# Conv stage of a two-layer network: four images side by side, tap tiles written back over three batches, logits in four column groups, last batch scaled by two engines

## The chip, the cores and the metric

The kernel runs on one core of one Trainium2 chip. The time is device microseconds from start to end of one execution. PE is the matrix engine (PEld its weight loads), DVE the vector engine, ACT the scalar engine, POOL the general one, SP the engine that issues most DMA transfers. A core has 16 DMA engines that carry the transfers of all queues.

## The reference

Two layers run after each other on x of 32 images, 128 channels, 56x56 pixels, all float32. The change lies in the first part of layer 0, up to the logits.

```python
x = jax.lax.conv_general_dilated(input, dw_kernel, (1, 1), ((3, 3), (3, 3)), feature_group_count=C, ...) + dw_bias
x = jnp.transpose(x, (0, 2, 3, 1))
mu = x.mean(-1, keepdims=True)
var = x.var(-1, keepdims=True)
x = (x - mu) / jnp.sqrt(var + 1e-06) * ln_gamma + ln_beta
xf = x.reshape(T, C)
logits = xf @ Wg + bg                 # 8 experts
topv, topi = jax.lax.top_k(logits, K) # K = 2
...
```

The tokens are then sorted by their weight, sent to experts of limited capacity (two matrix products with a gelu between), and added back. Layer 1 (a 3x3 depthwise convolution beside a scan over the pixels of each image, and two 1x1 convolutions) takes most of the time and is not changed.

## The kernel before, in words

The kernel is written for a framework that traces the program, orders each engine's instructions by a simulated greedy schedule, and places the semaphores itself. So the text of the program gives priorities, and the order on an engine can differ from it; once placed, each engine and each queue works strictly in that order. A pool with `bufs=n` gives each tile name n buffers; the (n+1)th use waits until the first is free. The conv stage has a pool `wp` (one buffer) and a pool `cp` (two, unless a tile says otherwise); in PSUM there are three buffers for `pc`, two for `p_in`, two for `p_xa`, one for `p_lg`.

The stage works on batches of four images (NB0 = 4, eight batches). A depthwise 7x7 convolution is turned into matrix products: two image rows (112 pixels, TT) of one channel lie along the partitions, 28 such row pairs (NP) and one of padding lie in the free dimension, and for each channel four 112x112 Toeplitz matrices made from the 49 taps are the weights.

- The taps are laid into `xt` among zeros and written to `taps_d` in DRAM (L337, L338). Only then is `xt` free for the first image.
- `fill(b, i)` (L341) loads one image into `xt` (L344, one buffer), turns it on PE, two rows at a time (L349), and copies four turned pairs at once on ACT into `slots2[b % 2]` (L351). All four images of batch 0 are filled ahead of the first convolution; those of batch b+1 are filled in the midst of batch b.
- `conv(b, c0)` (L353) does four channels: 16 matrix products (L379), each of them two passes in float32, and one addition of the bias on DVE (L383). The Toeplitz tiles `toep` hold two channels each and have five buffers. In batch 0 each is made from `raw`, which two transfers read from `taps_d` with overlapping rows (L361), by a copy on ACT (L368), and is written to `toep_d` in DRAM from POOL's queue (L369). `raw` shares the tag and the three buffers of `xa`. In batches 1 to 7 it is read from `toep_d` in one transfer (L371).
- `norm(b, i, q)` (L388) does seven of the 28 row pairs of one image, 16 times a batch, on the batch before the one being convolved: statistics over the channels on DVE (L396, L398), the root on ACT (L400), reciprocal and shift on DVE (L401, L403), seven scalings on ACT into `xa` (L406), gamma and beta on POOL (L409, L410), the store (L412), the turning of seven pieces on PE (L420), two copies on ACT into `xc_lg` (L422), then seven products with `xc_lg` as weights and the eight columns of `wg` streamed (L424), two passes each, and one addition of `bg` on DVE into the logits `lg` (L428).
- `top2(b)` (L430) finds the two best experts of a batch on DVE.

The last loop, at the end of the stage, mixes these: `conv` for all 32 groups of four channels, and between them the work list of norms, fills and one top2, spread evenly. The batch loop has one round more than there are batches: in it the last batch is normalized with no convolution beside it.

After the stage come the routing (to about 1.9 ms), the experts, and layer 1, which is bound by POOL's multiplications (L1330). Two lines of layer 1 serve only as prices: L1256 and L1284 are matrix products on four 64x64 quarters of the array.

## Time and profile before

Ten runs lie between 15733.27 and 15753.77 us.

| | us |
|---|---|
| median of ten runs | 15742.19 |
| profiled execution, its own time | 15740.14 |
| its span | 15738.4 |
| of it, conv stage up to the last logits | 1531 |
| ACT scalings L406 in the conv stage, 896 | 500.9 busy, 643 ns each |
| products of the logits L424, 1792 passes | 233.6 busy |
| Toeplitz copies L368, 64 | 60.0 busy, 943 ns each |

The profile gives for each engine its instructions with start and duration, and for idle time what ended it. In the rows "x" is a count, "<-" names what was waited for, and in the table of windows each engine has its busy time in a window followed by its number of instructions, then the TensorE clock granted (1 is full speed), the mean busy share of the 16 DMA engines, and what they moved. A matrix instruction's duration overlaps those of its neighbours, so a rate is read from the distance between starts. "q" after an engine's name is its sequencer, which issues transfers.

### The profile page before, as it was taken

To read this page: it belongs to the slowest core of one execution; us is meant where nothing else is said; L and a number is where in the kernel's file an instruction comes from. 1 tells how busy PE (TensorE), PEld (TensorE's weight loads), DVE (VectorE), ACT (ScalarE), POOL (GpSimd) and SP (SyncE) were. 2 spreads that over 40 slices of the span, in tenths; PEclk is the share of its full clock that TensorE was granted. 3 is DMA by queue.
4 is the path that set the end of the run, shared out by engine and by line. 5 is a ranking of instruction groups with operands and counts; after the bars stand their busy time and mean duration, and the time that the engine had idled before them with its cause. 6 is when DMAs were issued, how large, how long until landed. Compare 5 with 4: busy or idle time off the path is not lost. (4 is left out here: it accounts for less than half of the span.)

```text
span 15738.4 us, 249145 instructions
## 1 busy us (share of the span) xinstructions
PE 12846.1 (82%) x92981; PEld 7181.9 (46%) x92981; DVE 11109.1 (71%) x11254; ACT 10410.5 (66%) x20982; POOL 13461.5 (86%) x8122
## 2 busy tenths in 40 slices
PE   7996200003999989999999999999999999999998
PEld 7996100002777754444444444444444444444444
DVE  2655400000111149999999999999999999999999
ACT  4564200001444458888888888888888888888887
POOL 2443377777888879999999999999999999999999
PEclk9997555556999999999999999999999999999999
DMA  8785533333555545555555555555555555555555
GB/s 265 231 236 171 204 104 104 104 104 71 72 70 72 70 105 183 185 183 182 182 182 182 184 183 181 183 183 182 185 184 181 181 183 182 185 183 183 182 182 169
DMA packets 1239277, 2572.34 MB, mean 163 GB/s; under 512 B 139352, under 2 KB 676784, under 8 KB 1230384
## 3 DMA queue, kind: packets, MB, share of 16 engines
q1 hardware_dynamic: 1041584, 2361.95, 47.9%
q0 software_dynamic: 196480, 194.45, 7.3%
q8 instruction: 732, 11.99, 0.3%
q14 instruction: 481, 3.94, 0.1%
HBM read 2180.44 MB, written 375.43 MB: 162 GB/s over the span
## 5 line engine op out<-in xcount | busy, mean ns | idle before, releaser
L1330 POOL TENSOR_TENSOR db<-du,bb 128x896 f32<-128x896 f32 x3584 | 6843.6, 1940 | 0.1
L1343 ACT ACTIVATE da<-dt,aneg 128x449 f32<-128x449 f32 x7168 | 4540.2, 637 | 387.8 <-DVE r L1093 112.9
L1361 DVE TENSOR_TENSOR_SCAN da<-da,db 128x898 f32<-128x898 f32 x2240 | 4523.3, 2019 | 1.8 <-ACT da L1343 1.1
L1284 PE MATMUL py<-prod,ident 64*64 64x448 f32 x28672 | 3240.2, 548 | 178.7 <-DVE prod L1381 133.9
L1381 POOL TENSOR_TENSOR prod<-hs,cb 128x896 f32<-128x896 f32 x1344 | 2605.7, 1939 | 184.5 <-DVE r L1093 78.2
L1381 DVE TENSOR_TENSOR prod<-da,cb 128x896 f32<-128x896 f32 x2240 | 2440.2, 1089 | 202.7 <-DMA cb<-bc_d 88.3
L952 ACT COPY xc<-ept 128x512 f32<-128x512 f32 (+1 forms) x248 | 144.1, 581 | 2743.0 <-PE ept L950 2743.0
L858 POOL DMA_INDIRECT buf_d<-xg,slot x1568 | 1521.3, 970 | 484.9 <-issue 476.4
L910 POOL DMA_INDIRECT res_d<-ys,xb x984 | 1591.9, 1618 | 332.3 <-issue 287.1
L1361 DVE TENSOR_TENSOR_SCAN hs<-da,db 128x898 f32<-128x898 f32 x896 | 1785.7, 2014 | 0.1
L1284 PEld LDWEIGHTS py<-prod,ident 64*64 64x64 f32 x28672 | 1018.1, 132 | 1633.6 <-issue 883.1
L950 PE MATMUL ept<-ident,xb 128*128 128x128 f32 (+1 forms) x984 | 188.7, 274 | 1853.5 <-DMA xb<-buf_d 1853.5
L1124 PE MATMUL p_xm<-te,wk 128*128 128x448 f32 x3584 | 1395.4, 540 | 0.0
L902 DVE TENSOR_TENSOR ys<-py,b2t 128x512 f32<-128x512 f32 (+2 forms) x256 | 170.9, 670 | 1680.3 <-PE py L896 1663.3
L855 DVE COPY xg<-gate 128x28 f32<-128x28 f32 x56 | 11.5, 210 | 1749.1 <-DMA buf_d<-xg,slot 1749.1
L896 PEld LDWEIGHTS py<-w2t,hh 128*128 128x128 f32 x7872 | 936.2, 191 | 175.6 <-issue 113.4
L896 PE MATMUL py<-w2t,hh 128*128 128x128 f32 x7872 | 985.0, 278 | 0.3
L1124 PEld LDWEIGHTS p_xm<-te,wk 128*128 128x128 f32 x3584 | 671.7, 189 | 665.6 <-issue 567.7
L950 PEld LDWEIGHTS ept<-ident,xb 128*128 128x128 f32 (+1 forms) x984 | 124.6, 143 | 1857.0 <-issue 1856.6
L379 PE MATMUL pc<-xc,toep 112*112 112x112 f32 (+1 forms) x8192 | 940.2, 271 | 35.8 <-ACT toep L368 31.1
L1365 DVE TENSOR_TENSOR_SCAN hs<-da,db 128x449 f32<-128x449 f32 x896 | 927.3, 1077 | 0.8 <-POOL prod L1381 0.6
L1256 PE MATMUL p_l<-xh,dwd 64*64 64x224 f32 x16128 | 907.3, 352 | 22.1 <-ACT dt L1238 3.6
(240 smaller groups left out, 20138.2 us busy)
## 6 DMA issues: line engine op xcount, KB each, us to landing
bb<-bc_d SPq DMA_DIRECT2D x1792, 448.0 KB
cb<-bc_d SPq DMA_DIRECT2D x1792, 448.0 KB
toep<-toep_d SPq DMA_DIRECT2D x448, 392.0 KB
xg<-res_d SPq DMA_DIRECT2D x56, 1792.0 KB
buf_d<-zero SPq DMA_DIRECT2D x28, 2275.0 KB
xb<-buf_d SPq DMA_DIRECT2D x240, 260.0 KB
xt<-in_x SPq DMA_DIRECT2D x32, 1568.0 KB
res_d<-xa SPq DMA_DIRECT2D x128, 392.0 KB
```

What stands on the lines that cost most here:

```text
L379: nc.tensor.matmul(pc[:, c, :, lo:hi], lhsT=tp[c // 2][:, c % 2, 6 - 2 * o : 8 - 2 * o, :], rhs=s4[:, c, :, lo + o - 1 : hi + o - 1], star ...
L858: apart(nc.gpsimd.indirect_dma_start(out=buf_d[:, :], out_offset=bass.IndirectOffsetOnAxis(ap=slots[k][:, o + j : o + j + 1], axis=0), in_ ...
L896: nc.tensor.matmul(py[:n, j, :], lhsT=hh[:, k, j * 128 : j * 128 + n], rhs=w2t[:, k, :], start=k == 0, stop=k == KF - 1,)
L910: apart(nc.gpsimd.indirect_dma_start(out=res_d[:, :], out_offset=bass.IndirectOffsetOnAxis(ap=xb[:n, j, C + 1 : C + 2].bitcast(I32), axis= ...
L1124: nc.tensor.matmul(p[:, :CH1], lhsT=s["wk"][:, k, hs], rhs=d["te"][:, k : k + CH1], start=k == 0, stop=k == DC - 1 and not first,)
L1256: nc.tensor.matmul(d["p_l"][r][k * HD : (k + 1) * HD, : CH1 // 2], lhsT=s["dwd"][rs, t, rs], rhs=d["xh"][rs, dy + k * R : dy + (k + 1) * R ...
L1284: nc.tensor.matmul(ps[r][h * HD : (h + 1) * HD, :CH1], lhsT=lhsT(rs, h), rhs=rhs[rs, h, :], start=start, stop=stop,)
L1330: nc.gpsimd.tensor_tensor(dbv[i][:, :, 1:], st[g]["du"], units[u].pop("bb"), ALU.mult)
L1343: e = nc.scalar.activation(da[:, h * W1 : (h + 1) * W1], st[g]["dt"][:, h, :], AF.Exp, scale=s["aneg"][:, h, i : i + 1])
L1361: nc.vector.tensor_tensor_scan(hs, da, dbs[i], 0.0, ALU.mult, ALU.add)
L1365: half(u, h, nc.vector.tensor_tensor_scan(hs2[h][:, hh], da[:, hh], dbs[i][:, hh], 0.0, ALU.mult, ALU.add))
L1381: eng.tensor_tensor(w["prod"], w["hs"][0][:, :, 1:], w["cb"], ALU.mult)
```

## The change

Four things change in the conv stage.

- The two slot tiles become full 128-partition tiles `whole`. The second is not needed until batch 1 is filled, so it first holds the four images of batch 0 side by side (`begin`) and, behind them, the taps (`tapf`). `xt` serves batches 1 to 7. The zeros are set by DVE, not by POOL. The four image loads no longer wait for each other, and the first stands ahead of the write of `taps_d`. The loads of `wg` and of the rows follow behind them.
- `PACKED = (0, 44, 88, C)`: batch 0 builds all 64 tiles from `raw` but writes back only the first 22 (channels 0 to 43); batch 1 reads these 22 and builds 42 from `raw`, of which it writes back 22; batch 2 reads 44 and builds 20, writing all of them back. From batch 3 all are read. `raw` has its own name in the pool, with the pool's two buffers; `xa` keeps three.
- The logits: `wg` is padded with zeros to 32 columns and becomes the weights. The turned pieces lie in one tile `turns` (one buffer, an eighth piece of zeros). Four products, each of two pieces (224 columns), go to partitions 0, 32, 64 and 96 of one PSUM tile. ACT copies them to `lt`, PE turns them back in two transposes, and DVE adds `bg` with a rearranged view. `lg` has one column more and one buffer.
- In the last batch, three of the seven scalings of a norm (odd j) are done by DVE as one two-operation instruction.

```diff
@@ -309,8 +309,33 @@
             tc.tile_pool(name="po1", bufs=2, space=PSUM) as pot,
             tc.tile_pool(name="pl1", bufs=1, space=PSUM) as plg,
         ):
-            wg = wp.tile([C, E], F32, name="wg")
-            nc.sync.dma_start(out=wg, in_=a["L0_conv_Wg"])
+            SH = NP + 1
+            PAD = (HW + 2) * HW
+            whole = [wp.tile([128, C * NB0 * SH], F32, name=f"xc{i}") for i in range(2)]
+            slots2 = [t[:TT].rearrange("p (c j) -> p c j", c=C) for t in whole]
+            taps_d = dram.tile([C, TR * TS], F32, name="taps_d")
+            toep_d = dram.tile([TT, C, 8, HW], F32, name="toep_d")
+            tapf = whole[1][:, NB0 * PAD : NB0 * PAD + TR * TS]
+            nc.vector.memset(tapf, 0.0)
+            taps = tapf.rearrange("c (y x) -> c y x", x=TS)
+            dwk = a["L0_conv_dw_kernel"].rearrange("c o h w -> (c o) h w")
+            for y in range(7):
+                nc.sync.dma_start(out=taps[:, 7 - y, 52:59], in_=dwk[:, y, :])
+            begin = whole[1][:, : NB0 * PAD].rearrange("c (i n) -> c i n", i=NB0)
+            xt = wp.tile([C, PAD], F32, name="xt")
+            for v in (begin, xt.unsqueeze(1)):
+                nc.vector.memset(v[:, :, :HW], 0.0)
+                nc.vector.memset(v[:, :, HW + L :], 0.0)
+            nc.sync.dma_start(out=begin[:, 0, HW : HW + L], in_=x_d[0])
+            nc.sync.dma_start(out=taps_d, in_=tapf)
+            for i in range(1, NB0):
+                nc.sync.dma_start(out=begin[:, i, HW : HW + L], in_=x_d[i])
+            wg = wp.tile([C, 32], F32, name="wg")
+            nc.vector.memset(wg, 0.0)
+            nc.sync.dma_start(out=wg[:, :E], in_=a["L0_conv_Wg"])
+            turns = wp.tile([C, 8, TT], F32, name="xc_lg")
+            nc.vector.memset(turns[:, 7, :], 0.0)
 
             def rows(v, n, name):
                 t = wp.tile([TT, n], F32, name=name)
@@ -322,41 +347,31 @@
             lng = rows(a["L0_conv_ln_gamma"], C, "lng0")
             lnb = rows(a["L0_conv_ln_beta"], C, "lnb0")
 
-            taps_d = dram.tile([C, TR * TS], F32, name="taps_d")
-            toep_d = dram.tile([TT, C, 8, HW], F32, name="toep_d")
-            slots2 = [wp.tile([TT, C, NB0 * (NP + 1)], F32, name=f"xc{i}") for i in range(2)]
-            xt = wp.tile([C, (HW + 2) * HW], F32, name="xt")
-            nc.gpsimd.memset(xt, 0.0)
-            taps = xt[:, : TR * TS].rearrange("c (y x) -> c y x", x=TS)
-            dwk = a["L0_conv_dw_kernel"].rearrange("c o h w -> (c o) h w")
-            for y in range(7):
-                nc.sync.dma_start(out=taps[:, 7 - y, 52:59], in_=dwk[:, y, :])
-            nc.sync.dma_start(out=taps_d, in_=xt[:, : TR * TS])
-            nc.gpsimd.memset(xt[:, :HW], 0.0)
             def fill(b, i):
 
                 n = b * NB0 + i
-                nc.sync.dma_start(out=xt[:, HW : HW + L], in_=x_d[n])
+                if b > 0:
+                    img = xt
+                    nc.sync.dma_start(out=xt[:, HW : HW + L], in_=x_d[n])
+                else:
+                    img = begin[:, i, :]
                 for j0 in range(0, NP + 1, 4):
                     w = min(4, NP + 1 - j0)
                     p = pin.tile([TT, 4, C], F32, name="p_in")
                     for j in range(w):
-                        nc.tensor.transpose(p[:, j, :], xt[:, (j0 + j) * TT : (j0 + j + 1) * TT], ident)
+                        nc.tensor.transpose(p[:, j, :], img[:, (j0 + j) * TT : (j0 + j + 1) * TT], ident)
                     o = i * (NP + 1) + j0
                     nc.scalar.copy(slots2[b % 2][:, :, o : o + w], p[:, :w, :].rearrange("p j c -> p c j"))
+            PACKED = (0, 44, 88, C)
 
             def conv(b, c0):
 
                 tp = []
                 for c in range(c0, c0 + 4, 2):
                     t = cp.tile([TT, 2, 8, HW], F32, name="toep", bufs=5)
-                    if b == 0:
-                        raw = cp.tile([TT, 2, 8, TS], F32, name="raw", tag="xa", bufs=3)
+                    if b < len(PACKED) - 1 and c >= PACKED[b]:
+                        raw = cp.tile([TT, 2, 8, TS], F32, name="raw")
                         for r in range(2):
                             nc.sync.dma_start(
                                 out=raw[r * HW : (r + 1) * HW].rearrange("k c y x -> k c (y x)"),
@@ -366,7 +381,8 @@
                                 ),
                             )
                         nc.scalar.copy(t, raw[:, :, :, :HW])
-                        nc.gpsimd.dma_start(out=toep_d[:, c : c + 2], in_=t)
+                        if c < PACKED[b + 1]:
+                            nc.gpsimd.dma_start(out=toep_d[:, c : c + 2], in_=t)
                     else:
                         nc.sync.dma_start(out=t, in_=toep_d[:, c : c + 2])
                     tp.append(t)
@@ -401,38 +417,55 @@
                 nc.vector.reciprocal(rs, rs)
                 nm = cp.tile([TT, w], F32, name="nm")
                 nc.vector.scalar_tensor_tensor(nm, mv[:, :, 0], -1.0, rs, ALU.mult, ALU.mult)
-                xa = cp.tile([TT, 2 * 8 * TS], F32, name="xa", bufs=3)[:, : w * C].rearrange("p (j c) -> p j c", c=C)
+                xa = cp.tile([TT, w, C], F32, name="xa", bufs=3)
                 for j in range(w):
-                    nc.scalar.activation(
-                        xa[:, j, :], xv[:, :, j], AF.Identity, bias=nm[:, j : j + 1], scale=rs[:, j : j + 1]
-                    )
+                    if b == NB - 1 and j % 2:
+                        nc.vector.tensor_scalar(
+                            xa[:, j, :], xv[:, :, j], rs[:, j : j + 1], nm[:, j : j + 1], ALU.mult, ALU.add
+                        )
+                    else:
+                        nc.scalar.activation(
+                            xa[:, j, :], xv[:, :, j], AF.Identity, bias=nm[:, j : j + 1], scale=rs[:, j : j + 1]
+                        )
                 nc.gpsimd.tensor_tensor(xa, xa, lng.unsqueeze(1).to_broadcast([TT, w, C]), ALU.mult)
                 nc.gpsimd.tensor_tensor(xa, xa, lnb.unsqueeze(1).to_broadcast([TT, w, C]), ALU.add)
                 col = (b * NB0 + i) * TPI + q * w
                 nc.sync.dma_start(
                     out=res_d[col * TT : (col + w) * TT, :].rearrange("(k p) c -> p k c", p=TT), in_=xa
                 )
-                pl = plg.tile([TT, w, E], F32, name="p_lg")
                 for j0 in range(0, w, 4):
                     g = min(4, w - j0)
                     p = pot.tile([C, 4, TT], F32, name="p_xa")
                     for j in range(g):
                         nc.tensor.transpose(p[:, j, :], xa[:, j0 + j, :], ident[:TT, :TT])
-                    xc = cp.tile([C, 4, TT], F32, name="xc_lg")
-                    nc.scalar.copy(xc[:, :g, :], p[:, :g, :])
-                    for j in range(g):
-                        nc.tensor.matmul(pl[:, j0 + j, :], lhsT=xc[:, j, :], rhs=wg, start=True, stop=True)
+                    nc.scalar.copy(turns[:, j0 : j0 + g, :], p[:, :g, :])
+                pl = plg.tile([128, 512], F32, name="p_lg")
+                across = pl[:, : 2 * TT].rearrange("p (k t) -> p k t", k=2)
+                back = pl[:TT, 256:].rearrange("p (k m) -> p k m", k=2)
+                for j in range(4):
+                    nc.tensor.matmul(
+                        across[32 * j : 32 * j + 32], lhsT=wg, rhs=turns[:, 2 * j : 2 * j + 2, :], start=True, stop=True
+                    )
+                lt = cp.tile([128, 2, TT], F32, name="lt_lg")
+                nc.scalar.copy(lt, across)
+                for k in range(2):
+                    nc.tensor.transpose(back[:, k, :], lt[:, k, :], ident)
                 if i == 0 and q == 0:
-                    lgs[b] = cp.tile([TT, NB0 * TPI, E], F32, name="lg")
+                    lgs[b] = cp.tile([TT, NB0 * TPI + 1, E], F32, name="lg", bufs=1)
                 o = i * TPI + q * w
-                nc.vector.tensor_tensor(lgs[b][:, o : o + w, :], pl, bg.unsqueeze(1).to_broadcast([TT, w, E]), ALU.add)
+                nc.vector.tensor_tensor(
+                    lgs[b][:, o : o + 8, :].rearrange("p (j k) e -> p j k e", k=2),
+                    back.rearrange("p k (j m) -> p j k m", m=32)[:, :, :, :E],
+                    bg.unsqueeze(1).unsqueeze(2).to_broadcast([TT, 4, 2, E]), ALU.add,
+                )
 
             def top2(b):
 
                 n = NB0 * TPI
                 big = [TT, n, E]
                 cols = slice(b * n, (b + 1) * n)
-                lg = lgs.pop(b)
+                lg = lgs.pop(b)[:, :n, :]
                 oh = cp.tile(big, F32, name="oh", bufs=1)
                 first_b = first.unsqueeze(1).to_broadcast(big)
                 v = cp.tile([TT, 2, n], F32, name="v", bufs=1)
```

## The prediction

> **What bounds the kernel now.** I read the page first: span, busy shares, and the costliest group.
>
> ```profile
> span 15738.4 us, 249145 instructions
> L1330 POOL TENSOR_TENSOR db<-du,bb 128x896 f32<-128x896 f32 x3584 | 6843.6, 1940 | 0.1
> L1256 PE MATMUL p_l<-xh,dwd 64*64 64x224 f32 x16128 | 907.3, 352 | 22.1 <-ACT dt L1238 3.6
> ```
>
> The long last stage is set by POOL (0.1 us idle ahead of 3584 multiplications) and the change does not touch it. All that can move is the first 1531 us. I cut those at the first matmul of each batch (68, 247, 407, 572 and so on), and asked for the busy time of each engine between the cuts.
>
> ```profile
> core 0: us, PE busy (x) PEld busy (x) DVE busy (x) ACT busy (x) POOL busy (x), PEclk, DMA share, GB/s
> 0.00:68.00 68.00, 24.47 (x116) 18.16 (x116) 1.09 (x16) 24.24 (x39) 7.01 (x15) 0.82 0.59 184
> 68.00:247.00 179.00, 139.31 (x1140) 127.64 (x1140) 29.56 (x80) 74.43 (x96) 31.09 (x59) 0.90 0.93 320
> 247.00:407.00 160.00, 155.58 (x1476) 150.55 (x1477) 84.98 (x267) 95.71 (x190) 66.94 (x32) 0.98 0.82 239
> 572.00:738.00 166.00, 159.43 (x1479) 154.73 (x1478) 93.97 (x315) 97.64 (x192) 66.88 (x32) 0.95 0.79 233
> 1234.00:1386.00 152.00, 144.63 (x1365) 142.19 (x1363) 83.28 (x307) 79.02 (x160) 66.81 (x32) 0.94 0.73 205
> 1386.00:1531.00 145.00, 69.67 (x337) 62.60 (x336) 75.09 (x282) 78.55 (x160) 66.44 (x32) 0.51 0.17 45
> ```
>
> Four stages with four limits: 0 to 68 waits for images; batch 0 has the DMA engines at 0.93; batches 1 to 7 have PE full (159 of 166 us); the tail after 1386 has every engine half idle and is a chain of hand-overs.
>
> The timeline shows the start: each image waits until the one before has been turned.
>
> ```profile
> 11.79 0.33 SPq L344 DMA_DIRECT2D xt<-in_x  x1
> 18.58 4.63 PE L349 MATMUL p_in<-ident,xt 128*112 128x128 f32 x20 [18.58 <-DMA xt<-in_x]
> 25.56 0.37 SPq L344 DMA_DIRECT2D xt<-in_x  x1
> 41.10 0.36 SPq L344 DMA_DIRECT2D xt<-in_x  x1
> ```
>
> The waits of 68 to 247 show what batch 0 hangs on (total us, times, longest):
>
> ```profile
> ACT toep L368 <- DMA raw<-taps_d: 72.7, 43, 4.4
> PEld pc L379 <- ACT toep L368: 37.9, 36, 3.4
> ```
>
> The timeline near 919 us gives the rate of a matmul pair (load and matmul) in a full batch: 50 pairs of L379 in 5.00 us, and a pair of L424 every (0.67-0.178)/5 = 0.098 us, though its matmul has only 8 columns.
>
> ```profile
> 919.78 0.67 PEld L424 LDWEIGHTS p_lg<-wg,xc_lg 128*112 128x112 f32 x6
> 920.37 5.00 PEld L379 LDWEIGHTS pc<-xc,toep 112*112 112x112 f32 x50
> ```
>
> And the tail, its waits and one place of its timeline:
>
> ```profile
> ACT xa L406 <- POOL xa L410: 28.4, 7, 4.2
> ACT xc_lg L422 <- PE p_xa L420: 21.1, 8, 5.5
> ```
> ```profile
> 1515.20 2.07 POOL L410 TENSOR_TENSOR xa<-xa,lnb 112x896 f32<-112x896 f32 x1
> 1515.24 2.05 DVE L403 SCALAR_TENSOR_TENSOR nm<-mv,rs 112x7 f32<-112x7 f32 x1
> 1517.37 2.81 ACT L406 ACTIVATE xa<-xc,nm,rs 112x128 f32<-112x128 f32 x5 [4.21 <-POOL xa L410]
> ```
>
> L403 handles 7 elements, takes 0.14 us at its quickest in this trace, and here ends with the POOL instruction beside it.
>
> **The change, part by part** (minus is time won).
>
> *Start.* The first image no longer waits for the taps' round trip through DRAM, and the four images go out back to back. The tap loads are issued by 7 us as now, so image 0 leaves at about 7 and lands at 12 to 14 (it took 6.8 us from 11.79 to 18.58). Three more at 1.57 MB and the 320 GB/s of batch 0 are 15 us: landed by 27 to 29. The last one needs its 5 to 6 us of turning (62 to 68 now). Batch 0 begins at about 35 instead of 68: **-33**, bounds -26 and -38. The memsets move from POOL to DVE, which does 1.1 us of work here; covered.
>
> *Batch 0.* It began with 5 of 64 tap tiles ready and then took 2.55 us a tile (copies of L368 at 95.0 and 138.3 are 17 tiles apart), plus image loads in between. Per tile the DMA engines moved 444 KB of raw and wrote 392 KB back. Now only tiles 0 to 21 are written back, so bandwidth falls away as the limit. But raw loses its share of xa's three buffers and has the pool's two. One buffer's round is 0.8 us of issues on SP, landing, 0.94 us of copy, 0.03 to the next issue. Landing took 5.3 us under full load and 3.4 us where fewer were in flight (issued by 148.88, copied from 152.29). That is 7.1 or 5.2 us, by two buffers 3.55 or 2.6 us a tile. I take 3.1 for the 17 tiles with write-back and 2.6 for the 42 without: 17x0.55 + 42x0.05, less a little for image loads with emptier queues: **+8**. Bounds: 2.4 for all, -9; 3.1 for all, +32.
>
> *Batches 1 and 2.* 42 tiles of batch 1 and 20 of batch 2 are now raw: two SP issues for one, 0.94 us of ACT each, and 22 and 20 write-backs of 0.53 us on POOL's queue (POOL has 67 of 160 us of work, so its time is covered; L409 and L410 stand in line behind a write that waits for its copy). A slot is four channels, two tiles. Without raw it costs PE (160-9.7)/32 = 4.7 us in batch 1 (9.7 is the saving below). ACT has (95.7+5.7)/32 + 1.9 = 5.1 us a slot in the raw part, near the limit too, and SP's later loads and stores of xa queue behind a raw issue that waits for its buffer. The two raw buffers' round sets the slot: 0.8 + landing + wait for ACT + 0.97. Landing 4.2 (between 3.4 and 5.3, with write-backs beside half of them), wait 0.8 (between 0 and 2, half of the run of seven scalings, 3.9 us): 6.8 us, bounds 5.2 and 9.1. Five finished tiles in hand save 2.5 slots' excess. Batch 1: 11x4.7 + 21x6.8 - 2.5x2.1 = 190 against 160, **+30**, bounds 0 and +72. Batch 2, whose slot costs (165-9.7)/32 = 4.85: 22x4.85 + 10x6.8 - 5 = 170 against 165, **+5**, bounds -7 and +22.
>
> *Logits, batches 3 to 7.* Removed per norm: 14 pairs of L424. Between successive matmul starts these take 0.10 us each plus 0.19 of waiting at their two entries: 1.61 us. Added: 4 matmuls of 224 columns, two passes each. No row has four column groups over all rows; the nearest is L1256, same 224 columns, four 64x64 tiles at once: 907.3/16128 = 0.056 a pass, 8 passes 0.45. Serial, the other bound, is 0.19 a pass (eight untiled passes of L1304, 224 columns, take 1.68 us from the first start to the end of the last, which lasts 0.35), 1.52. Going into and out of the tiled form costs 0.09 each (by the starts in the last stage, a full-array matmul follows a 448-column L1284 after 0.465 us, where 0.375 lies between passes of a kind). Two transposes like L349: 0.22. A third wait, on the copy lt: 0.15. Sum about 1.0 us, saving 0.6, and 9.7 us a batch; over five batches **-48**. Bounds: 1.61-0.67 = 0.94 a norm, -75; serial, +40. ACT's new copy (224 elements; the 336 and 448 rows of L422 are 442 and 529 ns, so 0.355) costs 5.7 us a batch, beside ACT's 68 idle of 166; DVE's addition stays one.
>
> The Trainium skill, "TensorE: Matmul & The Clock Gate", part 3 (packing small matmuls), gives three column tiles a gain of 2.38, below L1256's 0.19/0.056 = 3.4. By it the eight passes would be an estimated 0.64 us, and this term -33 instead of -48; no row here shows column groups alone.
>
> *Tail.* ACT loses 3 of 7 scalings, 48x0.56 = 27 us, and gains 16x0.355 = 6 us. Its idle time (31 ahead of L406, 21 ahead of L422) I keep, and add 0.6 us a norm for lt behind a PE at half clock: 78.5-27+6+66+10 = 133 against 145: **-12**. The 48 scalings on DVE cost 0.27 each (L750, 128x128), 13 us in DVE's 70 idle. Bounds: no new wait, -25; halfway to the last rival's lock-out, +15.
>
> A rule speaks against this part: "SBUF — State Buffer", section "SBUF: two separate sides", says that a Vector instruction in a two-port mode and GpSimd lock each other out for a whole instruction. The row of L403 (0.14 at least, 1.07 at the median) agrees for two inputs; whether a one-input scaling is caught, no row shows. If each were, the tail would lengthen as in the last rival.
>
> **The sum.** -33+8+30+5-48-12 = -50, from the profiled execution's 15740.1 us (span 15738.4): 15690. That execution lies 2 us under the median of 15742.2, so **15692**. About 0.2% (31 us) can be told from no change.
>
> **Rivals.**
> 1. *Raw loads are hidden.* Prefetch covers them, each bound low: -33-9+0-7-48-12 = -109, **15633**. For: the scheduler moves loads ahead; against: two buffers. 0.20.
> 2. *Two raw buffers take over as the bound (slower).* With a round of c us per slot, batches 1 and 2 change by 26c-142 and the rest is -85; so it decides from c = 8.7. At c = 10 (landing 5.3, ACT 2.9) and batch 0 at +32: +57 **= 15799**. For: ACT's queue is in order, and image loads delayed raw landings to 11 us in batch 0 (issued by 139.10, copied at 150.21). Against: 3.4 us landings. 0.17.
> 3. *Column groups run one after the other:* 1.07x80 = +86, **15778**. Against: L1256. 0.08.
> 4. *The DVE scalings are locked out by POOL*, three times 2.07 a norm: DVE 75+13+99 = 187 against 145, +42 for -12: **15746**. 0.05.
>
> The forecast has 0.50 (15655 to 15725 by its own terms). Range 15630 to 15780: it takes in rivals 1, 3 and 4 and leaves out most of 2. Faster: 0.42 of the forecast's 0.50 and all of rival 1, less a little for errors they share, 0.60; slower: rival 2 and parts of 3 and the forecast, 0.22; the rest 0.18.
>
> **What would show it.** Start: first matmul of L379 near 35 us, four images issued before 13. Batch 0: no more than 0.85 DMA share after tile 22. Batch 1: 185 to 195 us, with ACT waiting for raw. Batches 3 to 6: 156 us each, matmuls of the logits 7 ns apart in fours. Tail: 133 us. It is wrong if batch 1 passes 215 us or stays at 160, or if the logits' passes start 190 ns apart.

## The result, and the profile after

The kernel became **slower by 0.4%: 15802.65 us**, median of 8 runs (15792.72 to 15820.37), against 15740.09 us for 28 runs of the kernel before. The ratio is 1.0040, with a 95% interval of 1.0032 to 1.0049. The forecast of 15692 and its range of 15630 to 15780 both miss it.

The page of the profiled run shows that the long last stage did its 3584 multiplications as before (1938 ns each, 1940 before). The loss lies in the conv stage.

```profile
span 15801.8 us, 248608 instructions
L1363 POOL TENSOR_TENSOR db<-du,bb 128x896 f32<-128x896 f32 x3584 | 6837.0, 1938 | 0.3 <-DMA bb<-bc_d 0.3
```

The table of windows of the kernel after, cut at the first matmul of batches 0, 1, 2, 3, 4 and 5 (33.4, 253, 480, 679, 836, 1001), and at the last convolution:

```profile
core 0: us, PE busy (x) PEld busy (x) DVE busy (x) ACT busy (x) POOL busy (x), PEclk, DMA share, GB/s
33.40:253.00 219.60, 153.15 (x1141) 138.27 (x1142) 32.04 (x88) 79.68 (x101) 11.82 (x22) 0.87 0.69 205
253.00:480.00 227.00, 173.88 (x1417) 149.42 (x1418) 86.97 (x286) 136.88 (x250) 78.18 (x54) 0.90 0.73 221
480.00:679.00 199.00, 167.12 (x1416) 148.75 (x1415) 99.12 (x333) 121.20 (x234) 77.29 (x52) 0.89 0.81 240
679.00:836.00 157.00, 150.90 (x1406) 136.56 (x1406) 88.37 (x279) 97.67 (x202) 67.00 (x32) 0.97 0.85 238
836.00:1001.00 165.00, 152.88 (x1416) 137.81 (x1415) 94.80 (x316) 101.31 (x208) 66.99 (x32) 0.97 0.82 235
1484.00:1602.00 118.00, 57.51 (x272) 30.50 (x272) 101.79 (x330) 59.86 (x128) 70.46 (x33) 0.53 0.21 55
```

Batches 0 to 2 have neither PE nor DMA nor ACT full: batch 1 takes 227 us with PE busy for 174 and ACT for 137, and the granted clock is 0.90, where it was 0.98 in the kernel before. No engine's work explains these batches; hand-overs do.

Cut by cut against the forecast (us; "moved" is after minus before, and "forecast" the term of the sum):

| | start | batch 0 | 1 | 2 | 3 | 4 | 5 | 6 | 7 | tail | last logits |
|---|---|---|---|---|---|---|---|---|---|---|---|
| before | 68.0 | 179.1 | 160.0 | 164.8 | 166.0 | 166.1 | 163.8 | 166.5 | 151.8 | 145.1 | 1531.1 |
| after | 33.4 | 219.5 | 227.5 | 199.0 | 156.6 | 164.9 | 167.2 | 167.5 | 148.4 | 118.3 | 1602.2 |
| moved | -34.6 | +40.4 | +67.5 | +34.2 | -9.4 | -1.2 | +3.4 | +1.0 | -3.4 | -26.8 | +71.1 |
| forecast | -33 | +8 | +30 | +5 | | | | | | -12 | -50 |

Batches 3 to 7 together moved by -9.6, where -48 was forecast. Of the 71 us at the last logits, 63 are left in the span; the rest of the program, which is the same, took 14207 us before and 14200 here, and between 14170 and 14215 in the variants below, the first four of their table aside.

The waits of batch 0 and of batch 1 in the kernel after (total us, times, longest):

```profile
ACT toep L383 <- DMA raw<-taps_d: 111.6, 56, 4.8
PEld pc L395 <- ACT toep L383: 61.9, 50, 4.1
```
```profile
PEld pc L395 <- ACT toep L383: 35.9, 29, 4.1
ACT xc_lg L441 <- PE p_xa L440: 29.4, 11, 4.7
ACT toep L383 <- DMA raw<-taps_d: 22.3, 13, 3.0
```

In batch 0 ACT waits for raw and PE for ACT, as in the kernel before but longer. In batch 1 PE waits for ACT's Toeplitz copies while ACT waits more for PE (29.4) than for raw (22.3). Such a wait for PE is no loss by itself: the variant pack0raw3 below, which rebuilds nothing in batch 1 and takes 157 us for it, has more of it.

```profile
ACT xc_lg L441 <- PE p_xa L440: 35.4, 11, 6.3
```

New in the kernel after is that Toeplitz copies, for which PE waits, stand behind it on ACT. That is the thread to follow.

The timeline of the start shows images 1 to 3 issued by 10.3 us and the first convolution at 33.38, as forecast; image 0 went out at 0.81 already, not near 7:

```profile
0.81 0.39 SPq L329 DMA_DIRECT2D xc<-in_x  x1
7.43 0.33 SPq L332 DMA_DIRECT2D xc<-in_x  x1
9.33 0.96 SPq L332 DMA_DIRECT2D xc<-in_x  x2
33.38 0.97 PE L395 MATMUL pc<-xc,toep 112*112 112x112 f32 x4 [1.54 <-ACT toep L383]
```

PE waits 1.2 us for image 1 (its turning begins at 15.26), and no longer for images 2 and 3: they are turned one after the other, and that takes until 32.6.

### The profile page after: what moved, and what is told of

It reads as the page before. It is cut to its first block, busy times and chain, and to the rows that moved or that the text cites. A ratio compares the mean times of both kernels' runs of the same rounds, so it can differ in the third digit from the quotient of the medians.

```text
span 15801.8 us, 248608 instructions
## 1 busy us (share of the span) xinstructions
PE 12831.8 (81%) x92469; PEld 7066.1 (45%) x92469; DVE 11137.3 (70%) x11309; ACT 10470.5 (66%) x21125; POOL 13446.2 (85%) x8120
## 5 line engine op out<-in xcount | busy, mean ns | idle before, releaser
L1363 POOL TENSOR_TENSOR db<-du,bb 128x896 f32<-128x896 f32 x3584 | 6837.0, 1938 | 0.3 <-DMA bb<-bc_d 0.3
L888 DVE COPY xg<-gate 128x28 f32<-128x28 f32 x56 | 11.7, 213 | 1743.8 <-DMA buf_d<-xg,slot 1743.8
L395 PEld LDWEIGHTS pc<-xc,toep 112*112 112x112 f32 x8192 | 901.8, 187 | 182.1 <-ACT toep L383 106.3
L430 POOL TENSOR_TENSOR xa<-xa,lng 112x896 f32<-112x896 f32 x128 | 267.6, 2090 | 822.6 <-ACT xa L427 777.4
```

The costliest lines, as they stand in the source:

```text
L395: nc.tensor.matmul(pc[:, c, :, lo:hi], lhsT=tp[c // 2][:, c % 2, 6 - 2 * o : 8 - 2 * o, :], rhs=s4[:, c, :, lo + o - 1 : hi + o - 1], star ...
L430: nc.gpsimd.tensor_tensor(xa, xa, lng.unsqueeze(1).to_broadcast([TT, w, C]), ALU.mult)
L1363: nc.gpsimd.tensor_tensor(dbv[i][:, :, 1:], st[g]["du"], units[u].pop("bb"), ALU.mult)
```

## The experiments

Each variant was timed once unless it says otherwise; single times of the kernel before scatter by 31 us, so the verdicts rest on the batch lengths of the profile. Those scatter too: in onlytail, which changes nothing before the last convolution, each batch is within 4 us of the kernel before, and batches 3 to 7 sum to 820.6 us against 814.2. The first four kernels were timed where the program behind the conv stage takes about 186 us longer, in the kernel before too, so their times are set beside 15926.56 us, the kernel before timed with them. All lengths are in one table:

| run | batch 0 | 1 | 2 | 3 | 4 | 5 | 6 | 7 | tail | time | before beside it |
|---|---|---|---|---|---|---|---|---|---|---|---|
| raw3 | 175.6 | 217.2 | 198.5 | 157.7 | 164.3 | 165.2 | 163.2 | 147.5 | 118.5 | 15942.63 | 15926.56 |
| pack0 | 233.3 | 159.4 | 162.5 | 168.9 | 163.8 | 167.6 | 165.0 | 148.1 | 118.4 | 15913.99 | 15926.56 |
| onlylogits | 179.2 | 159.3 | 167.1 | 164.8 | 164.5 | 165.5 | 165.4 | 148.8 | 144.1 | 15922.97 | 15926.56 |
| onlytail | 181.8 | 160.5 | 164.9 | 167.7 | 166.5 | 167.4 | 167.1 | 151.9 | 122.1 | 15911.37 | 15926.56 |
| dvecopy | 175.3 | 226.7 | 193.3 | 157.3 | 162.2 | 166.8 | 166.1 | 149.5 | 118.3 | 15765.33 | 15745.21 |
| pack0raw3 | 193.0 | 157.4 | 167.2 | 168.9 | 164.9 | 166.1 | 164.8 | 149.4 | 118.4 | 15695.64 | 15745.21 |
| pack0share6 | 194.4 | 152.4 | 162.4 | 162.6 | 158.7 | 163.6 | 160.9 | 145.4 | 118.2 | 15651.46 | 15745.21 |
| nowrite | 196.5 | 215.1 | 192.3 | 158.0 | 162.8 | 163.7 | 165.1 | 148.3 | 118.3 | 15749.87 | 15740.10 |
| writeonly | 196.4 | 167.9 | 176.5 | 167.1 | 163.5 | 163.7 | 163.6 | 149.1 | 118.4 | 15714.80 | 15740.10 |
| pack0share6old | 195.6 | 157.9 | 166.5 | 168.5 | 167.9 | 169.2 | 165.1 | 153.2 | 122.1 | 15704.93 | 15740.10 |
| pack0share7 | 200.8 | 152.3 | 162.0 | 161.8 | 164.0 | 163.8 | 163.8 | 145.1 | 118.2 | 15663.70 | 15740.10 |
| copyonly | 197.9 | 169.5 | 174.2 | 169.9 | 165.7 | 163.7 | 163.9 | 148.4 | 118.2 | 15699.73 | 15734.38 |
| loadsonly | 197.0 | 248.1 | 197.5 | 159.7 | 164.5 | 162.4 | 164.9 | 148.3 | 118.3 | 15795.85 | 15734.38 |
| after_toep6 | 216.1 | 232.3 | 192.7 | 152.2 | 162.3 | 161.7 | 161.9 | 144.8 | 118.4 | 15773.90 | 15734.38 |
| ahead0 | 193.7 | 200.6 | 182.1 | 158.8 | 163.4 | 166.0 | 167.4 | 149.7 | 118.2 | 15711.97 | 15716.70 |
| ahead1 | 195.1 | 194.2 | 171.1 | 160.5 | 164.0 | 165.1 | 165.8 | 150.1 | 118.3 | 15688.91 | 15716.70 |

### Are the two raw buffers the bound?

**raw3**: a third buffer for raw (paid for with one of the two of `lt_lg`).

```diff
-raw = cp.tile([TT, 2, 8, TS], F32, name="raw")
+raw = cp.tile([TT, 2, 8, TS], F32, name="raw", bufs=3)
```

> The changed kernel with three buffers for raw instead of two; lt goes from two buffers to one to make room. Theory A (the two raw buffers set the pace: in the changed kernel's trace each raw load is issued 0.03 us after the copy two tiles before it): a round of 5.05 us holds three tiles instead of two, so the part of batch 0 without write-backs goes from 2.55 to under 2 us a tile, and batches 0, 1 and 2 fall from 219, 227 and 199 us to about 165, 185 and 170; total about 15690. Theory B (the pace is that of the rebuilding itself, ACT's copies and the DMA traffic, whatever the buffers): the three batches shorten by less than 20 us together, total 15785 to 15800.

**pack0**: all tiles written back in batch 0, none rebuilt later, two raw buffers.

```diff
-PACKED = (0, 44, 88, C)
+PACKED = (0, C, C, C)
```

> The changed kernel with all 64 tap tiles written back in batch 0, two raw buffers as in the change. Theory A: batch 0 grows, because the write-backs lengthen the landings behind the same two buffers (64 tiles at 3.5 us: about 245 us against 219), batches 1 and 2 fall to the 157 to 165 us of the later ones; total about 15725. Theory B: the same for batches 1 and 2, but batch 0 stays near the 179 us that it took before the change, since its load is then the same; total about 15665.

Measured: raw3 takes batch 0 from 219.5 to 175.6 and leaves batches 1 and 2 at 217 and 198; pack0 takes 1 and 2 to 159 and 162 and makes batch 0 233. Neither theory holds throughout: A is right on batch 0 and wrong on batches 1 and 2 of raw3. So the two buffers are the bound in batch 0 only. In batches 1 and 2 the rebuilding costs 68 and 36 us, and the third buffer regains 10 and 0 of it.

What the third buffer does in batch 0 is seen in the starts of the copies. Away from image loads they are 3.25 us apart in the kernel after where the tile is written back and 2.67 where it is not; in raw3 2.47 and 2.15. Each of the three image loads stops them, with two buffers for 10.0, 11.7 and 11.7 us, with three for 9.9, 8.9 and 9.4. One stop in the timeline of the kernel after (tiles 30 to 33):

```profile
130.32 0.38 SPq L355 DMA_DIRECT2D xt<-in_x  x1
130.96 18.52 SPq L376 DMA_DIRECT2D raw<-taps_d  x8
133.81 0.94 ACT L383 COPY toep<-raw 112x896 f32<-112x896 f32 x1 [2.88 <-DMA raw<-taps_d]
...
140.00 6.57 PE L362 MATMUL p_in<-ident,xt 128*112 128x128 f32 x28 [2.89 <-DMA xt<-in_x]
141.14 1.57 ACT L364 COPY xc<-p_in 112x512 f32<-112x512 f32 x2 [6.40 <-PE p_in L362]
...
145.53 0.93 ACT L383 COPY toep<-raw 112x896 f32<-112x896 f32 x1
147.68 1.01 ACT L383 COPY toep<-raw 112x896 f32<-112x896 f32 x1
```

The image goes ahead of the next raw loads. The copy at 145.53 has no wait of its own: it stands on ACT behind the copies of the image's turned rows, and the first of these waits 6.40 us for PE, which waits for the image.

### Logits and tail by themselves

**onlylogits** is the kernel before with the changed logits, **onlytail** the kernel before with the changed scalings (`if b == NB - 1 and j % 2`); the hunks are those of the diff.

> The kernel before with the logits in four column groups alone. In the changed kernel batches 4 to 6 take 165 to 167 us, as before the change, though PE is 6 us less busy in each. Theory L1 (the new logits save PE about 0.4 us a norm, and PE then waits for toep loads instead): batches 3 to 6 stay at 163 to 167 us and waits of PE for DMA of toep appear, some 5 us a batch. Theory L2 (the saving is real and is lost to another part of the change): 157 to 160 us each, total about 15700. Tail: if the logits were what shortened it, about 125 us; if the scalings on DVE, about 145.

> The kernel before with the scalings of the last batch split between ACT and DVE alone. The tail after the last convolution was 145 us before and 118 in the changed kernel. If the split is what shortened it: 118 to 128 us, total 15715 to 15725. If it was the logits: 140 to 150, total 15735 to 15745. If GpSimd's instructions locked the DVE scalings out, over 150.

Measured: onlylogits leaves batches 3 to 6 at 165 us (165.6 before), onlytail brings the tail from 145.1 to 122.1. The split of the scalings thus makes 23 of the tail's 27 us; beside it the logits make the other 4 (122.1 against 118.2 in pack0share6old and pack0share6), alone they make 1 (144.1). In batches 3 to 6 of onlylogits PE waits 23.4 us for loads of finished tiles, as theory L1 said.

### Who copies, and who writes?

**dvecopy** is raw3 with the Toeplitz copies of batches 1 and 2 on DVE. **pack0raw3** joins pack0 and raw3. **pack0share6** is pack0 with raw back in xa's three buffers and a sixth Toeplitz buffer in the room won.

```diff
-nc.scalar.copy(t, raw[:, :, :, :HW])
+(nc.scalar.copy if b == 0 else nc.vector.tensor_copy)(t, raw[:, :, :, :HW])
```
```diff
-t = cp.tile([TT, 2, 8, HW], F32, name="toep", bufs=5)
+t = cp.tile([TT, 2, 8, HW], F32, name="toep", bufs=6)
...
-raw = cp.tile([TT, 2, 8, TS], F32, name="raw")
+raw = cp.tile([TT, 2, 8, TS], F32, name="raw", tag="xa", bufs=3)
```

> raw3 (three raw buffers, one lt) with the copies from raw to toep of batches 1 and 2 on DVE instead of ACT. raw3 brought batch 0 from 219 to 176 us, but batches 1 and 2 only from 227 and 199 to 217 and 198, so another limit holds there. Theory H (ACT's queue: a copy stands behind the norm's copies, which wait for PE, which waits for POOL and for the tap tiles): batches 1 and 2 fall to about 175 and 168 us. Theory D (the loads of the taps themselves, their DMA traffic and SP's queue): both stay above 195. Theory P (the copies only move into another queue that is as entangled; DVE also shares its port with POOL): 185 to 200.

> The changed kernel with all tiles written back in batch 0 and three raw buffers (one lt). With two buffers and everything written back (pack0) batch 0 took 233 us, with three and a third written back 176. If the buffers alone set the pace, about 178 us; if the DMA engines' rate does (836 KB a tile at 330 GB/s, 2.5 us), about 185. Batches 1 and 2 at 160 and 163 as in pack0, the tail at 118. Against the kernel before on the same chip: 34 less at the start, 27 less in the tail, 0 to 6 more in batch 0, some 5 less in the rest: faster by 55 to 65 us, ratio about 0.996.

> All tiles written back in batch 0, raw sharing xa's three buffers as before the change, and six toep buffers instead of five. Theory L1 (the saving of the new logits, 4 us of PE a batch, is given back in waits for toep loads, 5 us a batch in the changed kernel): the waits of PE for DMA of toep go to under 2 us a batch and batches 3 to 6 shorten from 165 to about 160 us. Theory L3 (PE's time does not fall, or the waits move elsewhere): they stay at 163 to 167.

With the copies on DVE batch 1 is no shorter (226.7), so theory H falls: that ACT carries them is not the cause. Theories D and P are not told apart (batch 1 lies where D put it, batch 2 with 193.3 where P did). pack0raw3 is about 50 us faster than the kernel before, and pack0share6 about 94, by one timed run each; batch 0 of pack0raw3, 193.0, is longer than either expectation.

**nowrite** (raw3's buffers, all tiles written in batch 0, batches 1 and 2 still rebuild but don't write) and **writeonly** (batches 1 and 2 load finished tiles, and write the change's 22 and 20 once more, into a spare tensor) take POOL's write-backs apart from the rebuilding.

```diff
-if c < PACKED[b + 1]:
+if b == 0:
     nc.gpsimd.dma_start(out=toep_d[:, c : c + 2], in_=t)
```
```diff
 nc.sync.dma_start(out=t, in_=toep_d[:, c : c + 2])
+if b < 3 and PACKED[b] <= c < PACKED[b + 1]:
+    nc.gpsimd.dma_start(out=spare_d[:, c : c + 2], in_=t)
```

> The changed kernel with three buffers for raw, all 64 tap tiles written back in batch 0 (as the variant whose batch 0 took 193 us), while batches 1 and 2 still rebuild the same 42 and 20 tiles from raw (two loads and one copy on ACT each) but write nothing. Only POOL's 42 write-backs of batches 1 and 2 are gone. Theory P (the rebuilding copy stands in an in-order queue between instructions that wait for PE, while PE waits for the copy): batch 1 at 205 to 220 us, batch 2 at 190 to 200, as with the writes (217.2 and 198.5). Rival W (a write in POOL's queue waits for its copy and holds up the gamma and beta behind it, and so the transposes and ACT): batch 1 at 158 to 170, batch 2 at 165 to 172.

> The opposite half: all 64 tiles are written back in batch 0 and batches 1 and 2 load finished tiles, but the tiles that the change writes back in those batches (22 and 20) are written from POOL's queue once more, to a spare tensor that nobody reads. No raw loads and no copies outside batch 0. Theory P: batch 1 at 157 to 163 us, batch 2 at 166 to 170. Rival W: the writes still stand in POOL's queue, though their tile comes from a load and not from a copy: batch 1 at 170 to 200, batch 2 at 175 to 195; if W needs the copy as what the write waits for, both runs fall between.

Without the writes batch 1 still takes 215.1 (217.2 with them); the writes alone cost 10.5 and 9.3 us against pack0raw3, more than theory P allowed (in batch 2 within what rival W said) and far from the 58 us by which nowrite's batch 1 exceeds that of pack0raw3 (157.4). The rebuilding itself is the greater part of the loss.

### The copy or the load?

**copyonly** loads a finished tile into the staging buffer in one transfer and copies it on ACT; **loadsonly** issues the raw loads, which nobody reads, beside the load of the finished tile, with no copy. Both write everything in batch 0 and have raw3's buffers.

```diff
+done = raw.rearrange("p c y x -> p (c y x)")[:, : 16 * HW].rearrange("p (c y x) -> p c y x", c=2, y=8)
+nc.sync.dma_start(out=done, in_=toep_d[:, c : c + 2])
+nc.scalar.copy(t, done)
```
```diff
-nc.scalar.copy(t, raw[:, :, :, :HW])
+nc.sync.dma_start(out=t, in_=toep_d[:, c : c + 2])
```

> All 64 tiles written back in batch 0, three staging buffers; in batches 1 and 2 the same 42 and 20 tiles are loaded finished, in one transfer, into the staging buffer and copied by ACT into the Toeplitz buffer. So the copy on ACT stays, and the pair of raw loads is gone. Theory P (the copy's place between instructions that wait for PE): batch 1 at 200 to 217 us, batch 2 at 185 to 195 (the variant with raw loads and copies had 215.1 and 192.3). Rival D (the two raw loads, their issues on SP and their landing): batch 1 at 157 to 170, batch 2 at 165 to 172.

> The other half: in batches 1 and 2 the raw loads of the 42 and 20 tiles are issued on SP as in the change, but nobody reads them; the finished tile is loaded beside them straight into the Toeplitz buffer, and there is no copy. That is three issues on SP and about twice the bytes a tile. Theory P: batch 1 at 157 to 185 us (the doubled traffic may cost some), batch 2 at 165 to 180. Rival D: batch 1 at 205 us or more, batch 2 at 185 or more.

> The changed kernel with a sixth Toeplitz buffer and nothing else (it still has two raw buffers and rebuilds and writes in batches 1 and 2). Theory P with slack: the copies can run half a slot earlier, batch 1 at 200 to 215 us instead of 227.5, batch 2 at 180 to 192 instead of 199.0. Theory P as a closed ring, where the copy's place in the queue decides and not its buffer: batch 1 at 220 to 230, batch 2 at 195 to 200. Batches 3 to 6 by both (L1): 158 to 163 us instead of 157 to 168.

Here theory P seemed to fall: 42 copies on ACT cost batch 1 only 12 us (169.5 against 157.4) and the 20 of batch 2 only 7, and loadsonly with 248.1 lies where rival D put it. But the latter can't be read as a cost of the raw loads alone, for with about twice the bytes a tile the DMA engines were nearly full, as its window shows beside that of copyonly (DMA share in the last column but one):

```profile
230.00:430.00 200.00, 153.51 (x1223) 130.80 (x1223) 78.18 (x257) 96.48 (x197) 66.64 (x32) 0.87 0.95 230
```
```profile
230.00:390.00 160.00, 141.99 (x1321) 128.38 (x1322) 70.05 (x258) 129.67 (x241) 66.86 (x32) 0.97 0.80 233
```

The timelines told what differed. For each of the 42 copies of batch 1 I took the time since its last load was issued, the wait for PE of the instruction directly ahead of it on ACT, and its own wait for the load:

| | median us since the load's issue | waits for PE directly ahead, sum | own waits for the load, sum |
|---|---|---|---|
| nowrite | 9.4 | 29.1 | 12.3 |
| copyonly | 5.6 | 0.0 | 9.0 |

The copies wait for their loads about as much in both, and in both some dozen of the 42 stand directly behind an `xc_lg` or `lt_lg`. But beside raw loads the framework's schedule had put most `xc_lg` right behind the scalings of their own norm, so that ACT stands there until POOL and PE have done theirs (eight of the eleven among the copies begin 0.7 to 3.0 us after POOL's last instruction); beside finished loads they come later (6 to 21 us after it) and ACT waits only 8.0 us for PE ahead of them, where it is 31.6 in nowrite. One such place in the timeline of nowrite:

```profile
335.99 1.65 PEld L395 LDWEIGHTS pc<-xc,toep 112*112 112x112 f32 x16 [3.27 <-ACT toep L383]
337.01 2.07 POOL L431 TENSOR_TENSOR xa<-xa,lnb 112x896 f32<-112x896 f32 x1
339.14 0.68 PEld L440 LDWEIGHTS p_xa<-ident,xa 112*128 112x128 f32 x7 [1.50 <-POOL xa L431]
339.14 0.89 PE L440 MATMUL p_xa<-ident,xa 112*128 112x112 f32 x7 [1.33 <-POOL xa L431]
339.78 0.53 ACT L441 COPY xc_lg<-p_xa 128x448 f32<-128x448 f32 x1 [3.84 <-PE p_xa L440]
340.21 0.94 ACT L383 COPY toep<-raw 112x896 f32<-112x896 f32 x1
341.20 3.06 PEld L395 LDWEIGHTS pc<-xc,toep 112*112 112x112 f32 x16 [0.69 <-ACT toep L383]
```

PE has done the two channels of a tile at 337.8 and needs the next. The tile's raw was issued 10.65 us before 340.21 (copies of this batch that did wait for their load began 3.0 to 5.5 us after its issue, so it most likely lay ready), and ACT was idle for 3.84 us. But the copy stands behind `xc_lg`, which waits for transposes on PE, which wait for POOL. The place of the transposes counts as well: they stand on PE ahead of the next convolution, and of the 1.9 us that PE is idle here 1.33 are their wait for POOL, so an earlier copy alone would not have saved these. Then the 16 weight loads take 3.06 us instead of 1.65.

**ahead0** and **ahead1** change the order: loads, copies and buffers are nowrite's, and an edge in the schedule puts each `xc_lg` of batches 1 and 2 behind the Toeplitz copies traced before it (`last` holds the latest of the batch being convolved). ahead1 also traces the tiles one group of channels earlier, in all batches, which moves their loads forward too.

```diff
+with tc.issue_after(last[b + 1].ins):
     nc.scalar.copy(turns[:, j0 : j0 + g, :], p[:, :g, :])
```

> The variant that rebuilds but writes nothing in batches 1 and 2 (215.1 and 192.3 us), with the same loads, copies and buffers; only ACT's order is changed: in batches 1 and 2 each copy of turned pieces (xc_lg, which waits for PE) is placed behind the Toeplitz copies of the four channels traced before it. Of the 42 copies of batch 1 one is then left directly behind an xc_lg, where there were eight, and three behind an lt_lg, where there were five. Theory P (the place in ACT's queue): batch 1 at 165 to 190 us, batch 2 at 170 to 182. Rival D (the raw loads themselves, on SP and in their landing): batch 1 at 205 to 217, batch 2 at 188 to 195.

> As the one before, and the tiles of each four channels are traced one group earlier, so that the edge holds for the next group's copies too; no copy of batch 1 is then left directly behind an xc_lg and three behind an lt_lg. Theory P: batch 1 no longer than in the one before, 162 to 188 us, batch 2 at 168 to 180. Rival D: 205 to 217 and 188 to 195.

Measured: batch 1 falls from 215.1 to 200.6 and 194.2, batch 2 from 192.3 to 182.1 and 171.1, both outside what rival D allowed; batch 1 stays above what P said. The waits for PE directly ahead of the copies fall from 29.1 to 8.5 and 3.9 us. So the order on the engines costs up to 21 us in each batch.

Through which link it costs them is only partly shown. PE's waits in batch 1 of nowrite, and of ahead1:

```profile
PE pc L395 <- ACT toep L383: 21.2, 25, 3.1
PE p_xa L440 <- POOL xa L431: 10.3, 7, 3.4
```
```profile
PE pc L407 <- ACT toep L385: 17.0, 17, 2.2
```

PE's wait for the copies themselves falls by 4 us (in batch 2 it stays, 4.7 and 4.5); the 10.3 us for POOL ahead of its own transposes are gone, for the edge moved these too: among the copies of nowrite seven of eleven norms have them 0.1 us after POOL's last instruction, in ahead0 and ahead1 all have them more than 3 us after it. And PE is busy for 159.4 us instead of 163.7 (in batch 2 for 152.7 instead of 164.5, at a granted clock of 0.96 instead of 0.90). That dvecopy, where no copy stands behind an `xc_lg`, gained nothing in batch 1 also speaks against the copy's place on ACT as the whole cause.

In batch 2 the order, with the 7 us of copying, accounts for the loss (171.1 against 167.2 without rebuilding). In batch 1 it is 21 of 58 us, and the copying 12. Another 14 are seen at its end in ahead1: the last matrix product ends 180.4 us after the batch's start, and the copies of the next batch's last image at 194.4, where pack0raw3 has them 1 us ahead of the last product. That image was issued on SP at 173.1 us (117.6 in pack0raw3), behind raw loads that wait for their buffers. In the kernel after, PE waits 8.5 and 10.6 us for images in batches 1 and 2, in pack0raw3 0 and 0.7; no run changed this alone. Some 11 us of batch 1 stay open.

after_toep6 adds a sixth Toeplitz buffer to the change: batch 1 is no shorter (232.3), batch 2 by 6 us (192.7), so slack in that buffer doesn't remove the loss.

### Where did the logits' gain go?

**pack0share6old** is pack0share6 with the old logits, **pack0share7** has a seventh Toeplitz buffer (five timed runs).

```diff
-t = cp.tile([TT, 2, 8, HW], F32, name="toep", bufs=6)
+t = cp.tile([TT, 2, 8, HW], F32, name="toep", bufs=7)
```

> The variant with all tiles written in batch 0 and six Toeplitz buffers (batches 3 to 6 of 162.6, 158.7, 163.6 and 160.9 us, total 94 us under the kernel before), but with the logits of the kernel before. Theory L1 (the column groups save some 4 us a batch, which five Toeplitz buffers took back as waits for their loads and six let through): batches 3 to 6 at 163 to 167 us, total 20 to 35 us above the variant with the new logits. Rival L2 (the sixth buffer alone made the gain, the column groups give nothing): batches 3 to 6 at 159 to 163, total within 10 us of it.

> All tiles written in batch 0, raw sharing the three buffers of xa as in the kernel before, and seven Toeplitz buffers in the room that this leaves. With six the batches 3 to 6 still waited 8 us for loads of finished tiles. If the seventh takes the rest: batches 3 to 6 at 157 to 161, total 95 to 110 us under the kernel before. If DMA or PE is the limit already with six: unchanged, 90 to 97 us under it.

The waits of PE for finished tiles in batches 3 to 6 of the kernel before, after, and pack0share6:

```profile
PE pc L379 <- DMA toep<-toep_d: 2.7, 5, 1.0
```
```profile
PE pc L395 <- DMA toep<-toep_d: 24.0, 15, 2.6
```
```profile
PE pc L395 <- DMA toep<-toep_d: 8.3, 9, 1.9
```

With five buffers a faster PE runs into its loads: its busy time falls from 159.4 to 152.9 us a batch, but 24 us of new waits come up in four batches. The -9.6 us of batches 3 to 7 is hardly a gain of the logits either: it is the -9.4 of batch 3, which with five Toeplitz buffers takes 157 to 161 us in every kernel that loads raw in batch 2 and 165 to 170 in those that don't; pack0raw3, with the new logits and five buffers, sums to 814.0, as the kernel before (814.2). A sixth buffer lets the gain through: batches 3 to 7 sum to 791.2 with the new logits and 823.9 with the old, 6.5 us a batch, by one run each. The old logits gain nothing by the buffer (823.9 against 814.2 in the kernel before). These batches are a little longer than theory L1 said, and the two totals lie 53 us apart and not 20 to 35, with 10 us of it in batches 1 and 2. The seventh takes the wait to 1.8 us and gains no more (798.5); at 76 us under the kernel before it misses both of its expectations. **pack0share7 beats both kernels**: 15663.70 us, a ratio of 0.9948 (0.9935 to 0.9962) to the kernel before. Whether six buffers are better than seven was not settled.

## Why the prediction was wrong, point by point

- **Start (-33).** Right in size, -34.6, partly by luck: the sum let image 0 leave at about 7 and the last landing set the end. Image 0 left at 0.81, and from 15.3 us on the turning of three images, 17.3 us in all, set it.
- **Batch 0 (+8, bounds -9 and +32).** The mechanism, the round of two raw buffers, was right (a third takes 44 us off in raw3); the term was mis-sized at +40.4. It can be split roughly. About 10 were forgotten: at the new start two tiles are ready, not the five of the kernel before, and 3 tiles at 3.3 us are missing. About 14 come from images: three loads stop the copies for 10.0, 11.7 and 11.7 us, where the kernel before had two such stops within the batch, of 9.8 and 9.5; the sum had taken "a little less for image loads". Tiles that are written back took 3.25 us apart from such a stop (3.1 forecast, +12 over 2.55 for 17), the others 2.67 (2.6 forecast, +5).
- **Batches 1 and 2 (+30 and +5).** This is the step that failed: "The two raw buffers' round sets the slot". raw3 shows that it doesn't: the third buffer regains 10 and 0 us of the 68 and 36. What the runs show in its place: the order on in-order engines, with `xc_lg` and its transposes, which wait for POOL, ahead of what the next convolution needs (up to 21 us in each batch, by ahead0 and ahead1; how much of it by the copy's place on ACT and how much by the transposes' on PE was not separated), the copying itself (12 and 7, by copyonly), in batch 1 some 14 at its end, with an image behind raw loads on SP's queue (seen in one timeline, not tried), and 11 open. The forecast counted busy time on ACT per slot (5.1 us) and treated its wait as up to half a run of scalings; it didn't ask what each copy stands behind and whom that waits for. "Covered" write-backs on POOL cost 2 to 10 us.
- **Rival 2** said 15799, within 4 us of the result, and isn't thereby right: its place was batches 1 and 2, where the third buffer regains almost nothing.
- **Logits (-48).** Two steps failed. The eight passes were priced at 0.45 us by L1256, with 0.18 for going in and out. In the trace the first starts at 905.03 and the next work on PE at 905.88, so 0.85 (the median of the 64 norms of batches 3 to 6 is 0.84). The passes were to start 7 ns apart in fours; in 60 of these 64 norms they start in pairs, 7 ns apart, and pairs follow each other after 0.21 and 0.12 us, some 0.085 a pass. In the four norms with full fours the next four start 0.375 us after the first (1104.085 to 1104.460), 0.094 a pass, and not 0.056. Against the 0.19 of an untiled pass that is a gain of 2.0 to 2.2, below the 2.38 by which the forecast's other figure, -33, was worked out. And the sum took PE's saving to be the batch's, though the finished tiles' loads were only just hidden: no gain that can be told from scatter with five buffers, and 33 us between old and new logits with six.

```profile
905.03 0.91 PE L447 MATMUL p_lg<-xc_lg,wg 128*32 128x224 f32 x8
905.88 1.23 PE L395 MATMUL pc<-xc,toep 112*112 112x108 f32 x10
```

- **Tail (-12).** Right in sign, measured -26.8, beyond its bound of -25. The mis-sized term is ACT's idle time, which the sum kept at 66 and raised by 10: it was 58 (118.0 less 59.9 busy), and the scalings' wait that ends with POOL fell from 28.4 to 6.1. Why it fell, no run shows. Rival 4's lock-out is there (below) but doesn't bound the tail.
- **What would show it.** The line "wrong if batch 1 passes 215 us" did its work. The "ACT waiting for raw" that was to confirm the forecast is in the profile (22.3 us) and was the wrong line to look at: 29.4 us of waits for PE stood beside it, with copies behind them.

## What to carry to other kernels

When work moves onto an in-order engine, busy time and buffers don't price it: list what each moved instruction will stand behind, and whether that waits, through other engines, for the one that needs the moved result; look at the order on that engine too. A stage that is bound by one engine hides only what it hides at its present speed; before a gain there is counted in full, look at which load arrives next to last, and give it a buffer. A total that agrees with a rival is no evidence for it; change the one thing that the rival names.

## What the hardware showed that was not expected

A one-input scaling on DVE that meets POOL's two-input instruction was held until that instruction ended. The timeline of the tail in the kernel after, and the row of its 48 scalings (shortest, median and longest ns):

```profile
1527.87 2.08 POOL L431 TENSOR_TENSOR xa<-xa,lnb 112x896 f32<-112x896 f32 x1
...
1528.11 2.00 DVE L423 TENSOR_SCALAR xa<-xc,rs,nm 112x128 f32<-112x128 f32 x1
```
```profile
L423 DVE TENSOR_SCALAR xa<-xc,rs,nm x48: 375/401/2244, 1497.5 to 1590.3; 112x128 f32<-112x128 f32 x48
```

The scaling that takes 0.40 us at the median took 2.00 and ended 0.15 us after POOL's did. It is no single case: 13 of the 48 took 1.89 to 2.24 us, each of them ended 0.15 us after an instruction of POOL, and none of the other 35 took more than 0.42. The forecast's 0.27 us, from a square tile of 128, was below the shortest one here (0.375).

PE's granted clock can halve for a few microseconds between stretches at full speed. In the place of nowrite shown above, 16 pairs of load and matmul took 1.65 us, and the next 16 took 3.06; PE had been idle for 1.9 of the 3.4 us between. The windows of the first 16 pairs, the gap and the next 16 pairs give the granted clock in the last column but two:

```profile
335.99:337.64 1.65, 1.65 (x16) 1.65 (x16) 1.54 (x8) 0.00 (x0) 1.57 (x2) 1.00 0.38 130
337.81:341.20 3.39, 1.46 (x12) 0.82 (x11) 0.00 (x0) 1.42 (x3) 1.28 (x1) 0.99 0.66 175
341.20:344.26 3.06, 3.06 (x16) 3.06 (x16) 0.00 (x0) 0.29 (x1) 0.00 (x0) 0.50 0.50 145
```

The lower clock thus cost 1.4 us here. That the gap brought it is not shown: the first 16 pairs came right after a wait of 3.1 us and ran at 1.00.
